# Issuing an image's first convolution sums behind the softmax terms on GpSimd: a two-layer attention and convolution kernel

## The chip, the cores and the metric

The kernel runs on one core of one Trainium2 chip. The metric is the device time of one execution, in microseconds (us). Five engines work at once, each on its own instructions in a fixed order: TensorE (PE in the profile) multiplies matrices, VectorE (DVE), ScalarE (ACT) and GpSimd (POOL) do elementwise work, and SyncE (SP) issues nearly all DMA transfers. An instruction that waits holds up everything behind it on its own engine.

## The reference

The input is 16 images of 56 x 56 pixels and 384 channels, in float32. Two layers follow each other, each added to its input:

```python
x = x + dilated_attention(group_norm(x), w_qkv, w_proj, b_proj)
x = x + depthwise_conv3x3(group_norm(x), sign(clip(w)))
```

The attention has 12 heads of 32 channels in three groups with dilations 1, 2 and 3. A pixel's query is compared with the keys of its 3 x 3 dilated neighbourhood, a softmax is taken over the nine scores, and the nine values are summed with those weights; a projection with `w_proj` follows. The convolution has one 3 x 3 filter of signs for each channel. The group norm (32 groups of 12 channels) needs the statistics of a whole image.

## The kernel before

**Tiles.** An image is cut into 7 chunks of 8 rows (448 pixels); there are 112 chunks, `m = 7*b + c`. Channels lie on the 128 partitions in three groups of 128. Three plans are made for each chunk: `plan_a` reads the image and takes statistics, `plan_b` is the attention, `plan_c` the convolution and the output.

**Order.** Time is counted in slices, nine for each chunk (`STEP = 9`). `at(when, order, piece)` files a piece of code under a slice; all pieces are then traced in the order of slices, and within a slice by kind, softmax first (`SOFTMAX, SCORE, STATISTICS, CONVOLVE, WEIGH, ...`). A scheduler then sets each engine's issue order: it may issue an instruction ahead of one that was traced earlier, when by its own estimate it is ready sooner. `in_one_go` and `keep_in_program_order` pin single instructions. The attention of chunk `m` starts at slice `9*m`, the convolution of chunk `m` at slice `9*(m+10)`. So the convolution of chunk `m` runs beside the attention of the chunks from `m+9` on. The convolution of an image's first chunk (`c == 0`) needs that image's new statistics; its pieces are filed one slice later than those of other chunks (`late = 1`), except `sum_g`.

**Attention of a chunk (`plan_b`).** `score` multiplies query and keys on VectorE (L516, tile `t`) and TensorE sums over channels (L501, `ps`). `softmax_1` to `softmax_5` turn the scores (L536), take the maximum, subtract (L540), exponentiate on ScalarE (L541), sum and divide (L545 to L547, tile `ew`). The weights are then split into three bf16 terms that together carry float32: the first is a cast on ScalarE (L555), the rest is formed on GpSimd: `rest` (L559), second term (L563), third term (L564), all in tile `e3` (`e` in the profile). `turn_weights` transposes the terms by a DMA issued on SyncE (L569) into `aT`. `weigh(i)`, i = 0 to 8, spreads three weights over the channels with three matmuls (L582, PSUM tile `pb_a`, one buffer), multiplies them with the values on VectorE (L589, tile `w`, four buffers), and sums on GpSimd: two additions of 128 x 1344 for each group (L597) and two of 128 x 448 (L600, L601) that give `y`. `out_project(j)` multiplies the three `y` with `w_proj` (L615, `po`). TensorE also computes queries, keys and values (L463) and much else in between.

**Convolution of a chunk (`plan_c`).** Two of the three channel groups go through TensorE (L710, `pc`). The third, called g, is made of nine products on ScalarE (`taps_g`, L761, tile `m`, three products in a tile) and sums on GpSimd: two of 128 x 1344 in `taps_g` (L767, for ky = 1 and 2), then `sum_g` with two of 128 x 448 (L772) and one more that adds the input (L775, tile `xg`). `turn` transposes the result for output four times for each chunk (L782), and ScalarE copies it (L787). In the last image (b = 15) VectorE does the g part instead (`taps_last`).

**Queues.** SyncE issues, in one order, the transposed weights (L569), the halo rows of keys and values (L477, L478), the loads of the convolution (`z`, L683; `xg`, L728), stores of `xd` (L437) and of the output (L790).

## Time and profile before

| What | Value |
|---|---|
| Time, median of 3 runs | 5328.02 us (5322.63 to 5328.53) |
| Time of the profiled execution | 5318.41 us |
| Its span, first to last instruction | 5316.7 us |
| TensorE busy / VectorE / GpSimd / ScalarE | 5131.6 / 4206.7 / 4255.0 / 2310.1 us |
| Mean granted TensorE clock | 0.981 |
| GpSimd L597, 128 x 1344 | 672 times 3083 ns |
| GpSimd L767, 128 x 1344 | 210 times, median 3048 ns |
| GpSimd L772 / L775, 128 x 448 | 210 times 1139 ns / 105 times 1137 ns |
| Transposing DMA L569, issue to landing | 112 times, median 4.0 us, at most 5.4 us |

The busy time of an engine is the time in which at least one of its instructions ran. In a timeline, a row gives start and duration in us, engine, line, operation, tile written and tiles read; what stands in brackets at the end is how long the engine was idle before the row, and what released it. In a table of stretches, each row gives the stretch, its length, each engine's busy time with the number of instructions, the granted TensorE clock (1.00 is full), the DMA engines' busy share and GB/s.

### The profile page before, as it was taken

What the parts mean: (1) busy time and instruction counts of PE and PEld (TensorE: products, weight loads), DVE (VectorE), ACT (ScalarE), POOL (GpSimd) and SP (SyncE); (2) the same over time, 40 slices, a digit from 0 to 9 for tenths busy, and PEclk for the clock granted to TensorE, in tenths of its full rate; (3) what the DMA queues carried; (4) which work ended last, traced back from release to release, by engine and by line L of the source; (5) the groups of instructions that cost most, each with busy time, mean ns of one, the idle gap of its engine ahead of it and who ended that gap; (6) DMA issues with size and microseconds to landing.
All of it is one profiled execution on the core that took longest, in us unless ns stands there. A gap on an engine that the chain in (4) does not pass through costs nothing. (4 is left out here: it accounts for less than half of the span.)

```text
span 5316.7 us, 75544 instructions
## 1 busy us (share of the span) xinstructions
PE 5131.6 (97%) x26885; PEld 2336.1 (44%) x26885; DVE 4206.7 (79%) x4125; ACT 2310.1 (43%) x4077; POOL 4255.0 (80%) x2950
## 2 busy tenths in 40 slices
PE   8999999999999999999999999999999999999976
PEld 4444444444444444444444444444444444444433
DVE  5887887878878788887888878788887888878764
ACT  3223444444444444444444444444444444444443
POOL 2677888888888888888888888888888888888881
PEclk8999999999999999999999999999999999999987
DMA  6434565556555565666555556555565555554545
GB/s 194 134 105 116 165 164 158 164 156 163 162 158 161 157 164 157 165 161 165 161 159 164 150 161 165 162 161 160 166 165 155 162 149 164 146 137 134 134 133 155
DMA packets 811630, 825.62 MB, mean 155 GB/s; under 512 B 360307, under 2 KB 801014, under 8 KB 811254
## 3 DMA queue, kind: packets, MB, share of 16 engines
q1 hardware_dynamic: 803270, 808.79, 55.5%
q10 hardware_dynamic: 7984, 12.00, 0.7%
q8 instruction: 213, 3.49, 0.3%
q14 instruction: 163, 1.34, 0.1%
HBM read 466.41 MB, written 231.21 MB: 131 GB/s over the span
## 5 line engine op out<-in xcount | busy, mean ns | idle before, releaser
L597 POOL TENSOR_TENSOR w<-w 128x1344 f32<-128x1344 f32 x672 | 2071.5, 3083 | 522.1 <-DVE w L589 500.8
L589 DVE TENSOR_TENSOR w<-pb_a,v 128x1344 f32<-128x1344 f32 x1008 | 1555.3, 1543 | 274.0 <-PE pb_a L582 235.8
L516 DVE TENSOR_TENSOR t<-pq,k 128x1344 f32<-128x1344 f32 x1008 | 1536.8, 1551 | 251.5 <-PE pq L463 251.0
L463 PE MATMUL pkv<-xn,wqkvT 128*128 128x448 f32 x3924 | 1565.9, 548 | 0.4 <-DVE xr L618 0.4
L463 PEld LDWEIGHTS pkv<-xn,wqkvT 128*128 128x128 f32 x3924 | 718.4, 190 | 668.8 <-issue 643.0
L615 PE MATMUL po<-y,wprojT 128*128 128x448 f32 x2016 | 835.2, 551 | 41.8 <-POOL y L601 32.4
L696 ACT ACTIVATE z<-z,mrz 96x448 f32<-96x448 f32 x840 | 578.4, 751 | 662.9 <-DMA z<-x1d 427.6
L463 PE MATMUL pq<-xn,wqkvT 128*128 128x448 f32 x1962 | 856.0, 572 | 0.0
L767 POOL TENSOR_TENSOR m<-m 128x1344 f32<-128x1344 f32 x210 | 640.1, 3048 | 152.9 <-ACT m L761 148.8
L501 PE MATMUL ps<-t,sel 128*32 128x448 f32 x6048 | 659.4, 545 | 7.9 <-DVE t L516 6.9
L761 ACT ACTIVATE m<-zg,ktap 128x448 f32<-128x448 f32 x945 | 555.5, 659 | 8.6 <-POOL xg L775 1.7
L615 PEld LDWEIGHTS po<-y,wprojT 128*128 128x128 f32 x2016 | 376.9, 192 | 400.8 <-issue 336.2
L710 PE MATMUL pc<-z,kdiag 96*32 96x440 f32 (+1 forms) x5040 | 515.5, 542 | 4.8 <-POOL z L698 4.4
L463 PEld LDWEIGHTS pq<-xn,wqkvT 128*128 128x128 f32 x1962 | 352.0, 194 | 327.3 <-issue 327.3
L582 PE MATMUL pb_a<-aT,spread 24*128 24x448 bf16 x3024 | 369.6, 360 | 71.7 <-DMA aT<-e 60.4
L618 DVE SCALAR_TENSOR_TENSOR xr<-po,bias,xr 128x448 f32<-128x448 f32 x336 | 228.5, 680 | 220.0 <-PE po L615 215.1
L601 POOL TENSOR_TENSOR y<-y,w 128x448 f32<-128x448 f32 x336 | 381.6, 1136 | 16.3
L600 POOL TENSOR_TENSOR y<-w 128x448 f32<-128x448 f32 x336 | 381.4, 1135 | 13.6
L473 ACT COPY v<-pkv 128x448 f32<-128x448 f32 x336 | 176.3, 525 | 487.8 <-PE pkv L463 470.0
L717 DVE TENSOR_TENSOR x<-pc,x 128x448 f32<-128x448 f32 x224 | 138.5, 618 | 276.1 <-PE pc L710 275.9
L582 PEld LDWEIGHTS <-spread 24*128 24x128 bf16 x3024 | 98.5, 91 | 560.9 <-issue 481.0
L473 ACT COPY k<-pkv 128x448 f32<-128x448 f32 x336 | 178.8, 532 | 381.0 <-PE pkv L463 381.0
(132 smaller groups left out, 4311.0 us busy)
## 6 DMA issues: line engine op xcount, KB each, us to landing
z<-x1d SPq DMA_DIRECT2D x570, 224.0 KB, 3.9
xr<-xd SPq DMA_DIRECT2D x112, 672.0 KB, 4.2
x1d<-xr SPq DMA_DIRECT2D x112, 672.0 KB, 3.2
xn<-xd SPq DMA_DIRECT2D x109, 672.0 KB, 4.6
xin<-in_x_dram SPq DMA_DIRECT2D x105, 672.0 KB, 7.2
xd<-xa SPq DMA_DIRECT2D x315, 224.0 KB, 3.4
out_dram<-osb SPq DMA_DIRECT2D x420, 168.0 KB, 3.5
x<-x1d SPq DMA_DIRECT2D x112, 448.0 KB, 8.2
```

What stands on the lines that cost most here:

```text
L463: nc.tensor.matmul(dst[:, :PX], wqkvT[:, cc, o0 : o0 + P], had["xn"][:, cc, :], start=(cc == 0), stop=(cc == NG - 1))
L501: return nc.tensor.matmul(had["ps"][32 * j : 32 * j + 32, :PX], sel[:, s0 : s0 + 32], tk, start=(issued[j] == 1), stop=(issued[j] == len(r ...
L516: nc.vector.tensor_tensor(t.rearrange("p k (r w) -> p k r w", w=W), q3, k3, ALU.mult)
L582: return nc.tensor.matmul(pb[:, kx, :PX].rearrange("p (s n) -> p s n", s=NSUB), spread[rows_of, v % 2, :], had["a"][rows_of, :, v // 8, :] ...
L589: nc.vector.tensor_tensor(w.rearrange("p k (r w) -> p k r w", w=W), pb[:, :, :PX].rearrange("p k (r w) -> p k r w", w=W), three(kv[1][g][m ...
L597: nc.gpsimd.tensor_tensor(w0, w0, w, ALU.add)
L601: nc.gpsimd.tensor_tensor(y, y, w0[:, 2], ALU.add)
L615: nc.tensor.matmul(po[:, :PX], wprojT[:, g, j * P : (j + 1) * P], had[f"y{g}"], start=(g == 0), stop=(g == NG - 1))
L696: nc.scalar.activation(z, z, AF.Identity, bias=mrz[:, j, q, 0:1], scale=mrz[:, j, q, 1:2])
L710: return nc.tensor.matmul(pcr[q * HD : (q + 1) * HD, :, lo:hi], kdiag[:, kx, j * NQ + q, :], rows(set_of(j, q))[:, :, lo + kx - 1 : hi + k ...
L761: nc.scalar.activation(rows(t[:, kx]), zp[:, ky : ky + ROWS, kx : kx + W], AF.Copy, scale=ktap[:, o : o + 1])
L767: nc.gpsimd.tensor_tensor(had["m"], had["m"], t, ALU.add)
```

## The change

For the first chunk of each image, the second 128 x 1344 addition (`taps_g` with ky = 2) and all of `sum_g` get an order on GpSimd: they are issued behind the third softmax term (L564) of chunk `m + 9`, which is traced in the same slices. It is an order of issue on one engine alone; no semaphore and no buffer is added. For other chunks, and in the last image, nothing is ordered.

```diff
+    last_term = {}
...
-            nc.gpsimd.tensor_tensor(term[2], r8, term[1], ALU.subtract)
+            last_term[m] = nc.gpsimd.tensor_tensor(term[2], r8, term[1], ALU.subtract)
...
+        def behind_softmax(wanted):
+            if c or not wanted:
+                return nullcontext()
+            return tc.issue_after(last_term[m + 9].ins)
+
         def taps_g(ky):
...
             else:
-                nc.gpsimd.tensor_tensor(had["m"], had["m"], t, ALU.add)
+                with behind_softmax(ky == 2):
+                    nc.gpsimd.tensor_tensor(had["m"], had["m"], t, ALU.add)
 
         def sum_g(kx):
             t = had["m"]
-            if kx < 3:
-                nc.gpsimd.tensor_tensor(t[:, 0], t[:, 0], t[:, kx], ALU.add)
-            else:
-                mid = had["xg"][:, 1 : ROWS + 1, :].rearrange("p r w -> p (r w)")
-                nc.gpsimd.tensor_tensor(mid, t[:, 0], mid, ALU.add)
+            with behind_softmax(True):
+                if kx < 3:
+                    nc.gpsimd.tensor_tensor(t[:, 0], t[:, 0], t[:, kx], ALU.add)
+                else:
+                    mid = had["xg"][:, 1 : ROWS + 1, :].rearrange("p r w -> p (r w)")
+                    nc.gpsimd.tensor_tensor(mid, t[:, 0], mid, ALU.add)
```

The scheduler runs again on the changed program, so other instructions move with it. The two built programs compare as follows. TensorE and VectorE have the same order. On GpSimd, in images 1 to 12 the order around the change is, before: w, m (L767), m (L772), w, m (L772), y, rest, y, e, xg, e; after: w, w, rest, y, e, y, e, m (L767), m, m (L772), xg (the last e is the third term, L564). In images 13 and 14, and in image 0, where the sums of the second chunk are interleaved too, the same sums likewise move behind the third term. On SyncE the transposing DMA moves ahead of one store of `xd` and one store of the output in images 1 to 12, and in image 0 a few loads change places. On ScalarE one copy of keys changes places with one product `m` of the image's second chunk; in image 0 the cast L555 and one copy move ahead of six products.

## The prediction

> **What bounds the kernel.** I read the busy shares first, then TensorE's waits, then the timeline around the commonest wait.

> ```profile
> PE 5131.6 (97%) x26885; PEld 2336.1 (44%) x26885; DVE 4206.7 (79%) x4125; ACT 2310.1 (43%) x4077; POOL 4255.0 (80%) x2950
> ```

> TensorE is the bound: 5316.7 - 5131.6 = 185 us of its span is idle. Only such idle time, or matmuls that run at a lowered clock, can be won. TensorE's own waits:

> ```profile
> engine line waited for: us in total, times, longest us
> PE pb_a L582 <- DMA aT<-e: 60.4, 20, 4.0
> PE po L615 <- POOL y L601: 32.4, 6, 12.3
> ```

> The reader is to see that the largest item is the transposed softmax weights, and the longest case 4.0 us. The timeline places them: six of 0.85 to 1.9 us lie before 401 us, then the start of each image has one: twelve of 3.91 to 4.01 us (images 1 to 12, at 811.11, 1132.62 and so on to 4340.05; sum 47.2 us), and 1.75 and 1.73 us in images 13 and 14 (4659.02, 4970.31). Those fourteen are chunk m + 9 of the change. Image 0 has none there. The waits for y lie in the tail (five after 5128 us, one at 501.68). One image start, image 5, on GpSimd:

> ```profile
> start us, us, engine line op out<-in xcount [idle before <-releaser]
> 2077.61 3.05 POOL L767 TENSOR_TENSOR m<-m 128x1344 f32<-128x1344 f32 x1
> 2080.74 1.39 POOL L772 TENSOR_TENSOR m<-m 128x448 f32<-128x448 f32 x1
> 2082.10 3.07 POOL L597 TENSOR_TENSOR w<-w 128x1344 f32<-128x1344 f32 x1
> 2085.12 1.14 POOL L772 TENSOR_TENSOR m<-m 128x448 f32<-128x448 f32 x1
> 2086.21 1.14 POOL L600 TENSOR_TENSOR y<-w 128x448 f32<-128x448 f32 x1
> 2087.31 1.17 POOL L559 TENSOR_TENSOR rest<-ew,e 112x512 f32<-112x512 f32 x1
> ...
> 2090.08 1.15 POOL L775 TENSOR_TENSOR xg<-m,xg 128x448 f32<-128x448 f32 x1
> 2091.18 1.17 POOL L564 TENSOR_TENSOR e<-rest,e 112x512 bf16<-112x512 f32 x1
> ```

> GpSimd has no idle time here, and four sums of the convolution stand between the weights and their third term. Then SyncE and TensorE:

> ```profile
> 2092.38 1.41 SPq L569 DMA_TRANSPOSE aT<-e  x1
> ```

> ```profile
> 2096.40 0.56 PE L582 MATMUL pb_a<-aT,spread 24*128 24x448 bf16 x3 [3.92 <-DMA aT<-e]
> 2096.89 3.93 PE L463 MATMUL pq<-xn,wqkvT 128*128 128x448 f32 x6
> ```

> The third term ends at 2092.35, the DMA goes out at once and lands 4.0 us later, and TensorE, ready at 2092.48, has waited. The six pq matmuls that follow take 3.93 us; elsewhere (2065.30) six take 2.52. The table of stretches says why (the clock is third from the end):

> ```profile
> 2096.40:2099.80 3.40, 3.40 (x7) 1.61 (x8) 1.56 (x1) 0.00 (x0) 3.24 (x3) 0.51 1.07 272
> 2099.80:2103.00 3.20, 3.20 (x27) 0.87 (x25) 2.14 (x2) 0.20 (x1) 1.04 (x1) 1.00 0.85 262
> ```

> [...]0.51 for 3.4 us after a 3.92 us gap, and all twelve long gaps are followed by it. [...]after 1.75 us at 4659.02 the clock also fell (0.76 over 7 us), after 1.73 us at 4970.31 it didn't (1.00). [...]

> ```profile
> 2078.99 2.14 DVE L547 TENSOR_TENSOR ew<-ew,sm 112x432 f32<-112x432 f32 x1
> ```

> ```profile
> 2129.50 0.60 DVE L547 TENSOR_TENSOR ew<-ew,sm 112x432 f32<-112x432 f32 x1
> ```

> The first fell into L767 (2077.61 to 2080.66) and ended 0.47 us after it; the second, one chunk later, was free.

> **The change, part by part, on image 5.** No instruction is added or removed; GpSimd's busy total stays.

> *Third term.* After the first w sum (ends 2077.65) GpSimd now comes to the second, which waits for VectorE's L589 (2077.58 to 2079.08). This is the situation of the next chunk, where no convolution sum stands in between:

> ```profile
> 2129.73 3.27 POOL L597 TENSOR_TENSOR w<-w 128x1344 f32<-128x1344 f32 x1 [1.03 <-DVE w L589]
> ...
> 2136.84 1.15 POOL L564 TENSOR_TENSOR e<-rest,e 112x512 bf16<-112x512 f32 x1
> ```

> There L547 begins just before the sum and takes 0.60, [...]and rest, y, e, y, e follow without a break; the third term ends at 2137.99. The two chunks stand 50.5 us apart at L589 (2128.09 - 2077.58). So the third term ends at 2137.99 - 50.5 = 2087.5, 4.9 us sooner than 2092.35. Step by step it is the same: sum 2079.2 to 2082.5, then 1.12 + 1.09 + 0.56 + 1.10 + 1.15 = 5.0. [...]

> *DMA.* SyncE now has the transpose ahead of a store of xd and one of the output, which it then holds from 2083.1 until 2088.9. Both were already free of hurry: xa has three buffers, osb two, the next osb copy (2090.15) uses the other one, and the next chunk's order on SyncE has the transpose ahead of xd as well. The halo rows (2095.69 before) follow at about 2092. aT lands at 2087.5 + 4.0 = 2091.5, before TensorE's 2092.48: 1.0 us of cover[...]. The stall goes whole; what comes last is TensorE itself.

> *Clock.* Without the gap the slow stretch goes. Over 7 us after each of the twelve gaps the mean clock was 0.63, 0.76, 0.63, 0.76, 0.76, 0.76, 0.76, 0.62, 0.76, 0.76, 0.76, 0.59; 7 x the sum of what is missing (3.45) = 24.2 us. In image 5 alone 7 x 0.24 = 1.7 us, against 3.93 + 0.56 less 2.52 + 0.36 = 1.6 from the matmuls.

> *The moved sums.* They take 3.05 + 1.14 + 1.14 + 1.15 = 6.5 us and now run from 2087.5 to 2094.0. Nobody waits for xg: the first L782 that reads it is at 2126.25. ScalarE's next product into m, at 2103.76, comes long after. Behind them stand the two w sums (2092.30 before, then 2094.0 to 2100.1) and y, y, done at 2102.4 instead of 2100.84. The third projection matmul pair of L615 needs it: before at 2108.03 + 1.6 = 2109.6, after 5.6 us sooner, 2104.0. Cover 1.6 us. GpSimd was idle for 5.1 us after 2100.84, which takes up the delay. VectorE's w has four buffers; its second w of the next group (2104.33 before, 2098.7 after) needs the buffer that the first of those two sums frees at 2097.0. Cover 1.7 us. I cost these at nothing; with the cover gone each us is one us for each image.

> *Small.* One key copy behind a product (0.66 us) meets a PSUM buffer with several matmul groups in between. TensorE already waits some 0.4 to 1.0 us for ScalarE's copies of v in sixteen places (9.4 us in all); with TensorE ahead at image starts I estimate 0.3 us more for each of 15 images, 4 us.

> *Images 13 and 14.* Before, rest stood behind two sums only; the third term ended at 4654.96. After: L589 ends 4643.42, then 0.14 + 3.27 + 5.0 gives 4651.8, landing 4655.8 against TensorE's 4657.27. Both stalls go, 1.75 + 1.73, and 1.7 us of slow clock in image 13: 5.2 us.

> *Image 0.* The third term there is not late (TensorE had 2.1 us to spare), but TensorE waits 1.33 us at 473.42, 1.62 at 484.66 and 2.09 at 501.68 behind a crowded GpSimd, and two slow-clock stretches follow. The order helps the first two and can lengthen the third. Bounds: 4 us gained to 4 us lost; I take 0.

> Sum: 47.2 + 24.2 + 5.2 - 4 = 72.6, say 72 us, on the profiled execution 5318.4 - 72 = 5246. The median of the runs lies 9.6 us above that execution, so 5328 - 72 = 5256.

> **The rivals.**

> *A, as worked out:* 5256, with 5246 to 5266 for image 0 and the small waits. Chance 0.76.

> *B, the DMA still comes late:* if [...]the landing takes 5 us instead of 4 (at most 5.4 was seen), 1 to 2 us of each stall stay and half of the clock dips with them: 12 x (1.5 + 1.2) = 32 us are kept, 5288. For it: a cover of only 1 us; against it: [...]over nine in ten landings are near 4.0 us. Chance 0.10.

> *C, nothing:* another input of pb_a was late too. TensorE's wait names the DMA, and VectorE, which frees its PSUM buffer, was done at 2091.97, so 5328. Chance 0.05.

> *D, slower:* the sums' delay lands on the projection. If GpSimd takes up nothing, y is late by the full 6.5 us (2107.3)[...]. L615 is due at 2104.0: a stall of 7.9, with 1.7 of slow clock 9.6 us for each image where 5.6 were removed, 12 x 4 = 48, so 5376. It decides from y later than 2104.0, and is a loss only beyond 2108. Against it: the computed 2102.4 and the 5.1 us of idle time behind. Chance 0.09.

> **Range and chances.** 5246 to 5288 holds A and B's middle. A measurement can tell about 0.2%, 10.7 us, from no change: A and B are faster (0.86), C the same (0.05), D slower (0.09).

> **What would show it.** In the profile after: third term some 4.9 us before TensorE needs aT, L547 near 0.60 at image starts, TensorE's wait for aT down from 60.4 to about 10 us (the six early ones), no stretch of 0.5 clock between 520 and 5100 us, POOL's busy total as before, no new wait of L615 for y before the tail. I am wrong if such a wait appears at image starts, or aT is still named there.

## The result, and the profile after

| | Before | After |
|---|---|---|
| Time, median of 4 runs beside each other | 5325.42 us (5322.63 to 5328.53) | 5254.84 us (5249.29 to 5261.22) |
| Ratio, with its 95% interval | | 0.9868 [0.9851, 0.9885] |
| Profiled execution, its span | 5318.41, 5316.7 us | 5261.22, 5259.5 us |
| Mean granted TensorE clock | 0.981 | 0.986 |

The change makes the kernel 1.3% faster. The medians differ by 70.6 us, the two profiled executions by 57.2, because the profiled execution of before lies below its four runs (beside the experiments below, the kernel before had medians of 5317 to 5320), and that of after is the slowest of its four. A second profile of the same order of issue (experiment 1) has a span of 5251.1 us, 65.6 less than before. So the gain is 57 to 71 us, and the forecast was 72.

The lines of the changed kernel stand one to ten lower: L582 is now L583, L547 is L548, L564 is L565, L615 is L616, L767 is L776. The busy shares of after:

```profile
PE 5106.2 (97%) x26885; PEld 2327.2 (44%) x26885; DVE 4188.3 (80%) x4125; ACT 2313.4 (44%) x4077; POOL 4256.5 (81%) x2950
```

GpSimd does the same work as before (4256.5 against 4255.0 us). The same 26885 matmuls keep TensorE busy for 25.4 us less. That fits the clock: 0.986 against 0.981 is half a percent of 5132 us, 26 us. The rest of the 57.2 is idle time. TensorE's waits, each with its total in us, how often, and the longest:

```profile
PE po L616 <- POOL y L602: 36.1, 6, 12.3
PE po L616 <- ACT v L474: 20.3, 28, 1.9
...
PE pb_a L583 <- DMA aT<-e: 10.9, 8, 2.1
```

The wait for aT fell from 60.4 to 10.9 us. Two others grew: for ScalarE's copies of v from 9.4 (16 times) to 20.3 (28 times), and for y from 32.4 to 36.1. Added up: 25.4 (busy) + 49.5 (aT) - 10.9 (v) - 3.7 (y) = 60.3 us. That is 3 us more than the 57.2 of the two profiles; these 3 us are the balance of smaller waits elsewhere, which grew.

The start of image 5 on GpSimd, in start, duration and what ended the idle time before:

```profile
2059.32 3.06 POOL L598 TENSOR_TENSOR w<-w 128x1344 f32<-128x1344 f32 x1 [2.19 <-DVE w L590]
2063.99 3.27 POOL L598 TENSOR_TENSOR w<-w 128x1344 f32<-128x1344 f32 x1 [1.60 <-DVE w L590]
2067.23 1.16 POOL L560 TENSOR_TENSOR rest<-ew,e 112x512 f32<-112x512 f32 x1
2068.34 1.14 POOL L601 TENSOR_TENSOR y<-w 128x448 f32<-128x448 f32 x1
2069.44 0.60 POOL L564 CAST e<-rest 112x512 bf16<-112x512 f32 x1
2070.01 1.13 POOL L602 TENSOR_TENSOR y<-y,w 128x448 f32<-128x448 f32 x1
2071.10 1.15 POOL L565 TENSOR_TENSOR e<-rest,e 112x512 bf16<-112x512 f32 x1
2072.22 3.03 POOL L776 TENSOR_TENSOR m<-m 128x1344 f32<-128x1344 f32 x1
```

Rest, y, e, y, e now follow the second w sum without a break, and the convolution's sum (L776) comes after the third term, as the step "third term" had it, with the forecast 3.27 us for the w sum. VectorE's division starts in the idle 1.60 us ahead of that sum, while no instruction runs on GpSimd, and takes 0.59 us:

```profile
2063.76 0.59 DVE L548 TENSOR_TENSOR ew<-ew,sm 112x432 f32<-112x432 f32 x1
```

It took 2.14 us before. At the starts of images 1 to 12 it took 2.11 to 2.14 us before and 0.58 to 0.61 after. In all of the trace of before, 45 of the 112 divisions begin while a 128 x 1344 addition runs on GpSimd: they take 1.04 to 3.15 us, and each ends 0.46 to 0.47 us after that addition. The 65 that begin while GpSimd runs nothing take 0.58 to 0.61 us.

SyncE, and then TensorE:

```profile
2072.28 1.53 SPq L570 DMA_TRANSPOSE aT<-e  x1
```

```profile
2075.51 1.71 PE L502 MATMUL ps<-t,sel 128*32 128x448 f32 x16
2077.16 0.36 PE L583 MATMUL pb_a<-aT,spread 24*128 24x448 bf16 x3
2077.45 2.52 PE L464 MATMUL pq<-xn,wqkvT 128*128 128x448 f32 x6
```

L583 has no bracket any more: TensorE didn't wait. The transposing DMA landed at 2076.27, 0.95 us ahead of the end of ps (2077.22). The six pq matmuls take 2.52 us instead of 3.93. In the table of stretches, the same 3.4 us from L583 on have a clock of 1.00 (third from the end) instead of 0.51, at almost the same DMA share (1.01 against 1.07):

```profile
2077.16:2080.56 3.40, 3.40 (x21) 1.44 (x21) 2.19 (x3) 0.00 (x0) 3.32 (x3) 1.00 1.01 261
```

### The profile page after: what moved, and what is told of

Same layout as the page of the kernel before. It is cut to its first block, busy times and chain, and to the rows that moved or that the text cites. A ratio compares the mean times of both kernels' runs of the same rounds, so it can differ in the third digit from the quotient of the medians.

```text
span 5259.5 us, 75515 instructions
## 1 busy us (share of the span) xinstructions
PE 5106.2 (97%) x26885; PEld 2327.2 (44%) x26885; DVE 4188.3 (80%) x4125; ACT 2313.4 (44%) x4077; POOL 4256.5 (81%) x2950
## 5 line engine op out<-in xcount | busy, mean ns | idle before, releaser
L616 PE MATMUL po<-y,wprojT 128*128 128x448 f32 x2016 | 838.5, 552 | 56.8 <-POOL y L602 36.1
L464 PE MATMUL pq<-xn,wqkvT 128*128 128x448 f32 x1962 | 833.9, 559 | 0.0
L776 POOL TENSOR_TENSOR m<-m 128x1344 f32<-128x1344 f32 x210 | 640.1, 3048 | 151.8 <-ACT m L769 147.6
L616 PEld LDWEIGHTS po<-y,wprojT 128*128 128x128 f32 x2016 | 377.4, 192 | 417.8 <-issue 336.5
L602 POOL TENSOR_TENSOR y<-y,w 128x448 f32<-128x448 f32 x336 | 381.5, 1136 | 16.3
L601 POOL TENSOR_TENSOR y<-w 128x448 f32<-128x448 f32 x336 | 381.7, 1136 | 13.7
L583 PE MATMUL pb_a<-aT,spread 24*128 24x448 bf16 x3024 | 368.4, 359 | 21.2 <-DMA aT<-e 10.9
L583 PEld LDWEIGHTS <-spread 24*128 24x128 bf16 x3024 | 98.3, 91 | 510.3 <-issue 489.2
```

The costliest lines, as they stand in the source:

```text
L464: nc.tensor.matmul(dst[:, :PX], wqkvT[:, cc, o0 : o0 + P], had["xn"][:, cc, :], start=(cc == 0), stop=(cc == NG - 1))
L583: return nc.tensor.matmul(pb[:, kx, :PX].rearrange("p (s n) -> p s n", s=NSUB), spread[rows_of, v % 2, :], had["a"][rows_of, :, v // 8, :] ...
L601: nc.gpsimd.tensor_tensor(y, w0[:, 0], w0[:, 1], ALU.add)
L616: nc.tensor.matmul(po[:, :PX], wprojT[:, g, j * P : (j + 1) * P], had[f"y{g}"], start=(g == 0), stop=(g == NG - 1))
L776: nc.gpsimd.tensor_tensor(had["m"], had["m"], t, ALU.add)
```

## The experiments

Three questions were open. Is the gain the moved transpose, or the shorter division? Is the clock a cost of its own? And where do the longer waits for v and y come from? Theory: TensorE gains its stall and the slow clock behind it, and then meets ScalarE's copies of v. Rivals are named at each run.

**1. add_alone.** Only the ky = 2 addition is ordered; the three small sums follow it by dependence. The order of issue on all engines is that of the changed kernel, so the run repeats its profile as well.

```diff
         def sum_g(kx):
             t = had["m"]
-            with behind_softmax(True):
+            with behind_softmax(False):
```

> Only the second 128 x 1344 addition is ordered behind the third softmax term; the order on the three small sums is taken away. They need that addition's result and follow it on the same engine, so the built order of all five engines is that of the changed kernel. Theory: the same time as the changed kernel, ratio to before 0.987 (0.985 to 0.989), and a second profile that shows how far TensorE's small waits for ScalarE's copies of v differ from one execution to the next (20 us in the changed kernel's profile, 9 in the one before; if that growth belongs to the change, near 20 again; if it is chance, anywhere from 5 to 25). Rival (the order on each of the small sums counts): nearer to before, 0.993 or more.

Measured: 5252.51 us, ratio 0.9873 [0.9859, 0.9886] (before beside it: 5319.73). The order on the addition does all of it. Waits for v were 16.3 us here, 20.3 in the other profile and 18.2 in run 6, always above the 9.4 of before, so their growth belongs to the change and their exact size to the single execution.

**2. sums_alone.** The other half: the ky = 2 addition stays in front, the small sums go behind. It separates the two parts of the gain that the step "third term" holds: the division L548 stays as long as before, while three of the four sums leave the path.

```diff
-                with behind_softmax(ky == 2):
+                with behind_softmax(False):
                     nc.gpsimd.tensor_tensor(had["m"], had["m"], t, ALU.add)
```

> The large addition stays in front[...]; only the three small sums (3.4 us) move behind the third term. Theory (what counts is when the third term ends against TensorE's need): large addition until 2080.7, the second w sum until 2083.9, third term at 2088.9 in the times of image 5, landing 2092.9 against 2092.5: a stall of about 0.4 us is left, too short for a clock drop. So 12 x 0.4 = 5 us above the changed kernel, ratio about 0.988. Rival (the gain comes from the softmax product that the large addition blocks, 2.14 instead of 0.60 us): most of the stall stays, over 2.5 us each, clock drops too, ratio 0.995 or more.

Measured: 5268.53 us, ratio 0.9906 [0.9892, 0.9919], 16 us more than run 1. On VectorE, and then TensorE, at the start of image 5:

```profile
2062.72 2.10 DVE L548 TENSOR_TENSOR ew<-ew,sm 112x432 f32<-112x432 f32 x1
```

```profile
2076.81 0.36 PE L583 MATMUL pb_a<-aT,spread 24*128 24x448 bf16 x3 [0.63 <-DMA aT<-e]
2077.11 2.52 PE L464 MATMUL pq<-xn,wqkvT 128*128 128x448 f32 x6
```

L548 is as slow as before, and still 3.3 of the 3.9 us of the stall are gone: the rival, that the shorter division is the gain, falls. What counts is how many sums stand ahead of the third term. The stalls that stay (0.62 to 0.69 us, but 1.65 in image 2, and 0.79 and 0.67 in images 13 and 14) are 9.0 us more in the wait for aT than in run 1 (20.0 against 11.0). The clock was 1.00 after every one of them, as it was in the trace of before after each of TensorE's 15 gaps of 0.41 to 1.03 us between 100 and 4980 us. Only 5 us above the changed kernel were expected, so in size this is a miss. What was not expected lies again at v: 22.9 us of waits against 16.3, and the clock fell behind the three longest of them (1.87, 1.88 and 2.02 us), which fits the 4.7 us more of TensorE's busy time. The profiled execution is the slowest of its four, 23.6 us longer than that of run 1, so these parts add up to more than the 16 us between the medians.

**3. rest_thrice.** The changed kernel, with the rest subtraction (same result each time) issued three times in the chunks of the twelve stalls. It puts back some 2.3 us ahead of the third term and tests the cover of 1.0 us.

```diff
-            nc.gpsimd.tensor_tensor(rest.rearrange(EIGHTS, k=8), e8, term[0], ALU.subtract)
+            for _ in range(3 if c == 2 and 2 <= b <= 13 else 1):
+                nc.gpsimd.tensor_tensor(rest.rearrange(EIGHTS, k=8), e8, term[0], ALU.subtract)
```

> The changed kernel with the subtraction that forms the rest issued three times instead of once in the third chunk of images 2 to 13 (the same result each time): 2 x 1.14 = 2.3 us more on GpSimd ahead of the third term. Theory (cover of 1.0 us): a stall of about 1.3 us comes back in each of twelve chunks, 16 us, and where the clock falls after it up to 1.7 us more (2 of 8 gaps of 1.7 to 1.9 us were followed by that before), 5 us in all: ratio 0.991 (0.989 to 0.994). Rival (GpSimd's idle time takes it up, or the DMA is no longer what TensorE waits for): ratio stays at 0.987.

Measured: 5269.84 us, ratio 0.9904 [0.9891, 0.9918], 17.3 us more than run 1. TensorE at the start of image 5:

```profile
2080.42 0.36 PE L584 MATMUL pb_a<-aT,spread 24*128 24x448 bf16 x3 [1.58 <-DMA aT<-e]
2080.71 2.52 PE L464 MATMUL pq<-xn,wqkvT 128*128 128x448 f32 x6
```

The third term came 2.5 us later and the stalls are 1.55 to 1.68 us: so about 1.0 us is absorbed and the rest is paid. Twelve stalls of 1.58 make 19 us. So aT was again what comes last. Only one of the twelve (1.68 us) was followed by a lower clock.

**4. before_warm4.** The kernel before, with four matmuls of 128 x 448 more (their result is overwritten) in each of the twelve gaps. They leave the late aT as it is and fill the idle time, and are meant to change the clock alone. Each appears as two matmul instructions in the profile (x8).

```diff
+WARM = 4
...
-            in_one_go([lambda kx=kx: copy(kx) for kx in (2, 0, 1)])
+            def keep_warm():
+                return nc.tensor.matmul(pb[:, 2, :PX], ident, wqkvT[:, 0, :PX], start=True, stop=True)
+
+            if i == 0 and c == 2 and 2 <= b <= 13:
+                for _ in range(WARM):
+                    tc.keep_in_program_order(keep_warm())
+                for kx in (2, 0, 1):
+                    tc.keep_in_program_order(copy(kx))
+            else:
+                in_one_go([lambda kx=kx: copy(kx) for kx in (2, 0, 1)])
```

> The kernel before with four more matmuls of 128 x 448 on TensorE in each of the twelve long gaps (images 2 to 13, third chunk), into the PSUM tile that the waiting matmuls overwrite: 4 x 0.84 = 3.4 us of a 3.9 us gap. Nothing else of the computation changes. Theory (two costs, the gap and the slow clock that its idle time brings on): matmuls after the gap run at full clock, 24 us less than before, ratio 0.9955 (0.994 to 0.9975), the wait for aT down to about 0.5 us each while the DMA lands no sooner. Rival (the matmuls after the gap are slow because DMA traffic is densest there, not because of the gap): they stay slow, ratio 1.000.

Measured: 5334.03 us, ratio 1.0028 [1.0021, 1.0034]: slower, a miss. At the gap itself all went as expected:

```profile
2097.84 3.27 PE L589 MATMUL pb_a<-wqkvT,ident 128*128 128x448 f32 x8
2101.83 0.37 PE L583 MATMUL pb_a<-aT,spread 24*128 24x448 bf16 x3 [0.71 <-DMA aT<-e]
2102.12 2.52 PE L464 MATMUL pq<-xn,wqkvT 128*128 128x448 f32 x6
```

pq is at 2.52 us. But TensorE's wait for v had grown:

```profile
PE po L625 <- ACT v L474: 34.2, 24, 3.9
```

The scheduler, which orders by its own estimates, had also moved work on other engines. In the second chunk of these images' convolution, five of ScalarE's products `m` now stood directly ahead of a copy of v:

```profile
2113.94 2.89 ACT L771 ACTIVATE m<-zg,ktap 128x448 f32<-128x448 f32 x5
2116.74 0.51 ACT L474 COPY v<-pkv 128x448 f32<-128x448 f32 x1
```

In the kernel before, that copy (at 2108.62) follows the four `z` directly, and no product stands in between. On GpSimd one convolution sum also went ahead of a w sum. The run measured several things at once.

**5. warm4_pinned.** The same, with that one order of before restored by hand: in the second chunk of images 1 to 12 the later products go behind the copies. (The expectation speaks of two products; the trace of run 4 shows five.) Without the extra matmuls this pin gives exactly the order of before. With them, ScalarE's copy `sT` still comes three `z` later than before, and a few loads of halo rows and of z change places on SyncE.

```diff
+                pin = None
+                if c == 1 and 1 <= b <= 12:
+                    pin = had["v_copy"] if 4 <= o < 7 else had["k_copy"] if o >= 7 else None
+                with tc.issue_after(pin.ins) if pin else ExitStack():
                     nc.scalar.activation(...)
```

> The four extra matmuls in each of the twelve long gaps again, with ScalarE's products of the image's second chunk ordered behind the copies of v and k as they stood before, since the scheduler had moved two products ahead of the copy of v, for which TensorE then waited. Theory (the slow clock costs time of its own): the copy of v is ready as before, TensorE comes to it 1.7 us sooner and waits 0 to 0.5 us, so 12 x 1.2 to 1.7 = 14 to 20 us less than before, ratio 0.9965. Rival (the slow clock costs nothing, since ScalarE's copy of v bounds that stretch anyway): ratio 1.000, the extra time found in waits for v.

Measured: 5295.09 us, ratio 0.9959 [0.9945, 0.9972] (before beside it: 5317.82): 22.7 us faster, though aT is as late as before.

```profile
2079.15 3.27 PE L590 MATMUL pb_a<-wqkvT,ident 128*128 128x448 f32 x8
2083.17 0.37 PE L584 MATMUL pb_a<-aT,spread 24*128 24x448 bf16 x3 [0.74 <-DMA aT<-e]
2083.47 2.52 PE L465 MATMUL pq<-xn,wqkvT 128*128 128x448 f32 x6
```

```profile
PE po L626 <- ACT v L475: 7.9, 13, 1.3
```

TensorE's useful matmuls start no sooner, they only run at full clock (2.52 us for the six pq, 3.93 in the kernel before). That the slow clock is a cost of its own is shown, and its size, 22.7 us, stands against the 24.2 of the step "clock". (The two profiles differ by 30.0 us; this one is the fastest of its five executions.) The two runs differ by 39 us, and their profiles show 26.3 us of it as waits for v (34.2 less 7.9) and 14.0 as TensorE busy time (5154.0 against 5140.0 us). This is what the moved order cost, above all the five products, 2.89 us of work ahead of one copy.

**6. without_image0** and **7. only_image0.** The change in all images but 0, and in image 0 alone.

```diff
-            if c or not wanted:
+            if c or b == 0 or not wanted:
```

> The changed kernel with the order left out for image 0. Theory (in image 0 nothing was late, and the order there costs more at the projection than it saves: 4.05 us saved up to the third chunk's weights, 6.8 us lost after it in the changed kernel's profile, 2.7 us net): 2 to 3 us less than the changed kernel, too little for the ratio alone (0.9868 instead of 0.9873), but the profile shows TensorE's wait for y near 502 us back at some 2 us instead of 6.2. Rival (image 0 gains as the others do): 3 us or more above the changed kernel, the wait for y unchanged.

```diff
-            if c or not wanted:
+            if c or b or not wanted:
```

> The order for image 0 alone, all else as before. Theory: 2 to 3 us slower than before, ratio 1.0004, and in the profile a wait of L615 for y of about 6 us near 505 us; all twelve long gaps stay. Rival: faster by 1 us or more.

Measured: 5253.06 us, ratio 0.9876 [0.9862, 0.9889], and 5322.32 us, ratio 1.0007 [0.9999, 1.0015]. Neither interval tells image 0 from nothing. The profiles do: TensorE at image 0, first in the kernel before, then in the changed one:

```profile
501.68 1.26 PE L615 MATMUL po<-y,wprojT 128*128 128x448 f32 x2 [2.09 <-POOL y L601]
```

```profile
505.08 1.86 PE L616 MATMUL po<-y,wprojT 128*128 128x448 f32 x2 [6.22 <-POOL y L602]
```

Up to the weights of the third chunk (484.82, where before it was 487.27) 4.1 us had been saved. After that 6.8 us are given back, 2.7 us lost in all: 4.1 by the longer wait for y, 1.7 up to 492.28, where TensorE waits 1.75 us for a copy of v (at 489.39), and 0.9 later, where matmuls run at a lowered clock (0.50 from 503.60 to 510.43). In run 6 the wait for y is 2.07 us, as before; in run 7 it is 6.24, and the twelve gaps are all there (60.5 us of waits for aT). The theory that image 0 costs a little is borne out by the profiles, not by the times.

**8. copies_ahead.** If the waits for v are what the change runs into, ordering ScalarE's copies ahead of the products must win them back. The rival: TensorE would wait for something else instead. Image 0 is left out as in run 6, and last_copy keeps the latest copies of k (0) and v (1).

```diff
+                with tc.issue_after(last_copy[1].ins) if j == 0 and c == 1 and 0 < b < B - 1 else ExitStack():
                     nc.scalar.activation(z, z, AF.Identity, ...)
...
+                pin = None
+                if b and c in (1, NCH - 1):
+                    pin = had["v_copy"] if 4 <= o < 7 else had["k_copy"] if o >= 7 else None
+                with tc.issue_after(pin.ins) if pin else ExitStack():
                     nc.scalar.activation(...)
```

> The changed kernel without image 0, and on ScalarE the copies of v and k ordered ahead of the later products (and of one normalisation z) in the second and last chunk of an image's convolution. Theory (TensorE's waits for v, 16 to 20 us in the two profiles of the changed order, come from products and z that stand before the copy when the load of xg is late): these waits fall to under 8 us, ratio 0.985 (0.983 to 0.9865), some 8 to 12 us under the changed kernel. Rival (products that are held back delay GpSimd's sums and so the third term of the next chunks): waits for aT or y grow, ratio 0.9875 or more.

Measured: 5239.35 us (5233.64 to 5241.96), ratio 0.9849 [0.9836, 0.9863]: 13.7 us less than run 6, and the fastest of all versions. TensorE's waits:

```profile
PE po L617 <- POOL y L603: 32.0, 5, 11.3
...
PE pb_a L584 <- DMA aT<-e: 10.9, 8, 2.1
...
PE po L617 <- ACT v L475: 2.5, 8, 0.7
```

15.7 us of waits for v went (18.2 to 2.5), 13.7 us came out as time. The waits for aT and y did not grow against run 6 (11.6 and 32.9 there), so the rival falls. With the new order on ScalarE the scheduler also moved sums on GpSimd; TensorE and VectorE kept their order.

**9. copies_before.** The same order on ScalarE in the kernel before, without the change on GpSimd.

> The kernel before, with the same ScalarE orders as copies_ahead and no order on GpSimd. Theory (nine or so of TensorE's waits for v at the start of an image exist only once the long gap is gone; before, only the waits in the last chunk of an image's convolution, 6.7 us, are there to be won): 4 to 7 us less than before, ratio 0.999, all twelve long gaps stay. Rival (the waits for v are worth the same with and without the change): 12 us or more, ratio 0.9977 or less.

Measured: 5313.98 us, ratio 0.9995 [0.9987, 1.0003]. Waits for v fell to 2.3 us (7 times), aT stayed at 60.5; 3.3 us gained where 4 to 7 were expected; the interval does not tell it from nothing. The copies of v were no cost worth naming while TensorE stood still at each image start.

## Why the prediction was right

The forecast of 72 us holds against 57 and 66 between profiles and 70.6 between medians. What is won was forecast well: 50.7 us at aT and 25.9 by the clock, where 49.5 and 25.4 were measured. What is lost again was set too low, at 4 us: it is 17.7 us in the one profile of this order and 9.8 in the other. That the medians still come within 2 us of the forecast is in part luck: the four runs of before lie 6 to 8 us above that kernel's medians beside the experiments, and beside 24 of its runs the same order (run 1) gained 67.2 us. By its steps:

*Third term and DMA: right.* The w sum took 3.27, L548 0.59, and the third term came early enough; the cover was 0.95 us where 1.0 was forecast, and run 3 shows the same 1.0 from the other side. Two landings were late all the same, 5.80 and 5.05 us after the issue instead of 4.0, with stalls of 0.89 us (1129.35) and 0.17 (2393.90). The prediction had called "aT is still named there" a sign of being wrong: the sign came up at two of the fourteen places. The waits for aT lost 49.5 us; forecast were 47.2 + 1.75 + 1.73 = 50.7.

*Clock: right.* 24.2 us, and 1.7 in image 13, were forecast; TensorE's busy time fell by 25.4, and run 5, with the clock alone, won 22.7. One sign failed: no stretch of half clock was forecast between 520 and 5100 us, and the profile has one at 2947.5, behind the longest wait for v below, and more from 5033 on, in the tail. The profile of run 1 has none from 520 to 4980 us.

*The moved sums: right.* At the start of image 5 y ends at 2087.49, and the third pair of L616 begins at about 2088.8. The cover was 1.3 us where 1.6 was forecast; no wait for y appears at the image starts from image 1 on.

*Small waits: too small.* The step put "0.3 us more for each of 15 images, 4 us" on ScalarE's copies of v. Measured were 10.9 us in one profile of this order and 6.9 in the other. The places differ from one execution to the next. The longest of the changed kernel lies in the last chunk of an image's convolution; TensorE, then ScalarE:

```profile
2937.75 4.78 PE L464 MATMUL pkv<-xn,wqkvT 128*128 128x448 f32 x12
2942.36 2.42 PE L616 MATMUL po<-y,wprojT 128*128 128x448 f32 x6
2944.71 0.36 PE L583 MATMUL pb_a<-aT,spread 24*128 24x448 bf16 x3
2946.99 4.22 PE L616 MATMUL po<-y,wprojT 128*128 128x448 f32 x6 [1.91 <-ACT v L474]
```

```profile
2941.64 0.81 ACT L740 ACTIVATE zg<-xg,mr 128x504 f32<-128x504 f32 x1 [1.64 <-DMA xg<-x1d]
2942.49 4.03 ACT L769 ACTIVATE m<-zg,ktap 128x448 f32<-128x448 f32 x7
2946.42 0.52 ACT L474 COPY v<-pkv 128x448 f32<-128x448 f32 x1
```

ScalarE had stood waiting for the load of xg, and seven products were queued ahead of the copy that TensorE needed. pkv begins 3.9 us ahead of zg here (2941.64 - 2937.75); in the kernel before, in the same chunk, it was 2.3 (2968.35 - 2966.07), and the wait 0.29. TensorE had come forward and the load had not. Here the clock fell too, to 0.50 from 2947.54 to 2950.96: the six L616 took 4.22 us. What was missed is that 5.6 us won by TensorE at the image start are 5.6 us less in hand for whatever runs on another engine's time.

*Image 0: within its bounds.* Taken at 0 with 4 us either way; the profiles show 2.7 lost, most of it by the wait that "can lengthen".

*The rivals.* B asked for 1 to 2 us left of each stall, which was an estimate: its late landing is real, but two of fourteen stalls are left, both under 1 us. (B's sum takes 1.2 us for half of a clock dip; half of 24.2 / 12 is 1.0, so 30 us and not 32.) C fell with the stall itself. D needed y later than TensorE: it is so in image 0 alone, which was not among D's twelve. Its stall of 7.9 us, 4.6 more than a y at 2107.3 gives, was an estimate that no run showed.

## What to carry to other kernels

When the bounding engine waits for a short chain on a crowded engine, put that chain first and let the work that nobody waits for follow; the price to check is the slack of what moves back, here 1.3 us, and places where the chain was not late (image 0) are better left alone. Count the slow clock after a gap beside the gap: here, after twelve gaps of 3.91 to 4.01 us, it was half as much again (24.2 us beside 47.2). And list, before the change, what the bounding engine reads from the others in the next tens of us: what it won there had to be met by ScalarE's copies, and ordering these ahead was worth another 13.7 us, while without the change it was worth next to nothing. Last, compare the order of issue on every engine after an edit, not only on the one edited: in run 4 products that moved on ScalarE cost more than the filled gaps won.

## What the hardware showed that was not expected

Whether TensorE's clock fell after a gap went with where the gap lay, and not with its length alone. Counted between 520 and 4980 us in ten profiles of this study (both kernels and all runs but only_image0), with the mean clock in the 7 us after each of TensorE's gaps of 1.2 us and more: after 31 gaps of up to 1.65 us it never fell; after 21 of 1.68 to 3.22 us it fell 12 times, with 1.68 us among the falls and 3.08 not; after all 26 of 3.84 us and more it fell. The kernel before has fourteen of these gaps: the twelve of 3.91 to 4.01 us (mean clock 0.59 to 0.76), one of 1.75 (0.76) and one of 1.73 (1.00).

```profile
3722.45:3725.86 3.41, 1.86 (x8) 0.56 (x6) 1.81 (x2) 3.41 (x7) 0.55 (x1) 1.00 0.60 112
3725.86:3729.27 3.41, 1.88 (x5) 1.06 (x6) 0.88 (x2) 1.90 (x4) 3.41 (x2) 1.00 0.11 34
3729.27:3732.69 3.42, 3.42 (x28) 0.94 (x27) 1.31 (x2) 0.99 (x2) 3.42 (x2) 1.00 0.88 257
```

```profile
1443.10:1446.52 3.42, 1.74 (x17) 0.56 (x10) 1.28 (x3) 0.00 (x0) 3.26 (x3) 1.00 1.05 228
1446.52:1449.93 3.41, 3.41 (x6) 1.15 (x4) 1.17 (x1) 0.00 (x0) 3.33 (x3) 0.50 1.08 308
```

The longer gap is split into 1.55 and 1.53 us of idle time in two steps, and the clock stays full. The shorter one lies in a single step, and the next step runs at half. Counted over the eleven traces between 520 and 4980 us: of 14276 steps at full clock, 14215 had less than 1.68 us of idle time, and none of these was followed by half clock; all 37 with more than 2.02 us were; of the 24 in between 15 were. Of 72 steps at half clock, the 51 with at most 0.20 us of idle time were followed by full clock, and the 21 with 0.35 us or more by another step at half. The kernel before alone has 13 steps at full clock that half clock followed, with 1.75 us of idle time in one and 2.02 to 3.41 in twelve; in its other 1275 it was at most 1.92. So in these traces the clock of the next step went with the idle time within a step. That is what was counted: no run varied this idle time alone, and why the 24 cases in between fall both ways stays open. The two sizes of dip in the step "clock", a mean of 0.76 or of about 0.62 over 7 us, are one and two steps at 0.50: eight of the twelve gaps are followed by 3.41 us of it, four (from 809.53, 1451.23, 3055.50 and 4338.91) by 6.83.
